# Second attention's last sums, m2, output block and first filters put in other places of a C2f-attention kernel

## The chip, the cores and the metric

The kernel runs on one NeuronCore of a Trainium2 chip. The core has five engines with queues of their own: TensorE (PE, matrix products into PSUM), VectorE (DVE) and ScalarE (ACT) for elementwise work, GpSimd (POOL), and SyncE (SP), which here only issues DMA transfers. The engines meet through semaphores. Each runs its own instructions in the order in which the program lists them, so the place of an instruction in its engine's list matters as much as what it computes. The metric is the device time of the whole program in microseconds (us).

## The reference

The input is eight images of 512 channels by 32 x 32 pixels in float32. A group norm over 32 groups is followed by a block with two inner stages, and the block's input is added at the end:

```python
def bot_attention(x, qkv_w, rw, rh):
    b, c, h, w = x.shape
    hw = h * w
    qkv = conv2d(x, qkv_w, 0).reshape(b, 3, HEADS, HD, hw)
    q, k, v = (qkv[:, 0], qkv[:, 1], qkv[:, 2])
    r = (rw + rh).reshape(1, HEADS, HD, hw)
    logits = jnp.einsum('bhdi,bhdj->bhij', q, k + r) * HD ** (-0.5)
    a = jax.nn.softmax(logits, axis=-1)
    out = jnp.einsum('bhij,bhdj->bhdi', a, v)
    return out.reshape(b, c, h, w)
...
t = cbs(x, cv1_w, cv1_bn, 0)
ys = [t[:, :C], t[:, C:]]
for i in range(N):
    yi = ys[-1]
    z = cbs(yi, m_cv1_w[i], m_cv1_bn[i], 1)
    z = bot_attention(z, m_qkv_w[i], m_rw[i], m_rh[i])
    z = jax.nn.silu(bn_eval(conv2d(z, m_cv2_w[i], 0), m_cv2_bn[i]))
    ys.append(yi + z)
return cbs(jnp.concatenate(ys, axis=1), cv2_w, cv2_bn, 0)
...
x = x + _L0_conv_ref(_gn(x), L0_conv_cv1_w, L0_conv_cv1_bn, L0_conv_cv2_w, L0_conv_cv2_bn, L0_conv_m_cv1_w, L0_conv_m_cv1_bn, L0_conv_m_qkv_w, L0_conv_m_rw, L0_conv_m_rh, L0_conv_m_cv2_w, L0_conv_m_cv2_bn)
```

Here N = 2 stages, C = 256 channels, 4 heads of 64, and `cbs` is a convolution with batch norm and SiLU. `m_cv1_w` is a 3 x 3 convolution, all others are 1 x 1.

## The kernel before

**Pairs and stages.** Images are worked on in four pairs (p = 0 to 3); call their images a and b. A pair goes through two stages n = 0 and 1. In each, a 3 x 3 convolution (`conv3x3`, in Winograd form, both images at once) is followed, for a and then for b, by the products for q, k and v ("projection"), the attention, and `m2` (the 1 x 1 convolution behind the attention, with SiLU and the addition of the stage's input). After stage 1 the output convolution cv2 of a and of b follows as a Strassen product with blocks `a1, a1_more, a2, a3` and `b1, b1_more, b2, b3`. The attention of b is called the second attention of its stage.

**Filling PE.** The group norm and the first convolution (cv1) of the next pair are done inside the present pair: cv1 of the next pair's image a within stage 0's first attention and m2, cv1 of its image b around stage 0's second attention. cv1 is cut into pieces: `begin`, `go_on`, then `rest(0)` to `rest(3)`. In pair 0 (`direct`) it is plain, with 16 profile rows (7.0 us) for each of four output blocks; later it is a Strassen product, with `begin` of 8 rows (3.5 us), `go_on` of 16 (7.1 us), and four `rest` of 8 rows. Each fp32 product counts as two rows in the profile. In the last pair parts of cv2 (`parts_of`) stand there instead.

**Attention.** `attention_fast` runs over four groups g (a 128-channel block and a half of 512 query columns), each with four pairs of key blocks: PE makes logits (`l_ps`, L960), ACT their exponentials (`pt`, L964), DVE adds up the exponentials (`acc`, L978 and L980), PE multiplies by v (`av_ps`, L994). A group's result is evacuated by ACT and a DVE addition (`z`, L1001 and L1002). The sums over partitions (`s_ps`) go through memory in `sums` and `spread`, and DVE multiplies `z` by the reciprocals `rs` (`scale`, L1066). For the second attention of stage 0 (`at_once=True`) the last group's sums are made directly in PSUM (`last_sums`, L1028), with the reciprocal of a whole 128x512 tile on DVE (L1111).

**Hooks.** The dictionary `behind` holds work to be put behind the additions of a given place: the key (g, j) is the j-th pair of group g, an integer g its first pair, NG = 4 the end of the last group and NG + 1 the place behind the last sums. The two tuples `NORM_A` and `NORM_B` say at which of these places the next pair's group norm takes its next step; the steps are statistics of the four input blocks (DVE), their mean over groups (`gm_ps`, a small PE product, L661), the inverse deviation (`gv_ps`, `gr`, L680, then three GpSimd steps up to `shift`, L681, L737, L738), and the normalisation on ACT (`x`, L744):

```python
        NORM_A = ((0, 2), (0, 3), (1, 1), (1, 2), (1, 3), 2, (2, 1), (2, 2), (2, 3), 3)
        NORM_B = ((0, 1), (0, 2), (0, 3), (1, 1), 2, (2, 1), (2, 2), (2, 3), 3, (3, 1), (3, 2), (3, 3))
```

**Preparations in pair 0.** Filters for stage 1's convolution are turned into Winograd form by `make_u` (DVE, ACT, and stores issued on GpSimd), four blocks (oc, k) from `load_late`'s taps; `more_u` steps through them, and `u_new` are the results. The position sums rw + rh are made by `make_r` (`r_new`, L206) and stored: for n = 1 in stage 0's first attention, for n = 0 in stage 1's. Convolution inputs of image a for the next stage are made in pieces by `tiles_in`; `tiles_later(1)` and `tiles_later(2)` are such pieces (`v_new`, stored by GpSimd, L1745).

**What sets the order.** A scheduler lists the instructions of each engine in program order; `tc.issue_after(x)` puts what follows behind instruction x. PSUM has three two-bank slots with the tag "big" (for logits, norm means, sums, m2 and the convolution) and one slot for `av_ps`; an operation waits until a slot's last reader is done. In `conv3x3`, ACT copies half of each result (`c_m`, L609) and DVE adds and subtracts (`c_t`, L610 and L611, to `z`, L642). In `b3` the last call, `finish(3)`, issues the output block's ACT operations (`c_out`, L460), whose stores GpSimd issues (L1263).

Of the kernel before, what the change touches and what calls it, by code (L numbers as in the profile page):

```python
# [61 lines left out]
def kernel(  # L62
# [137 lines left out]
    def make_r(n, raw):  # L200
        if raw is not None:
            nc.gpsimd.tensor_copy(planes(rw_sb[:, n]), natural(raw))
        for c in range(NM):
            for half in range(NH):
                r = act.tile([P, ROWS, F], F32, tag="t", name="r_new", bufs=4)
                nc.gpsimd.tensor_tensor(  # L206
                    r, rw_sb[:, n, c].unsqueeze(1).to_broadcast([P, ROWS, F]),
                    rh_sb[:, n, c, ts(half, ROWS)].unsqueeze(2).to_broadcast([P, ROWS, F]), ALU.add,
                )
                nc.gpsimd.dma_start(r_dram[n][c][:, ts(half, HALF)], r.rearrange("p h w -> p (h w)"))  # L210
# [245 lines left out]
    def stages(act, small, ps_big, ps_av, n_pt):  # L456
# [8 lines left out]
        shifted = [None]  # L465
# [97 lines left out]
        def conv3x3(n, vs, u_of, z, groups=G, summed=None):  # L563
# [10 lines left out]
            for oc in range(NM):  # L574
                dst = z[:, oc].rearrange("p g x -> p (g x)").rearrange("p (t r w) -> p r t w", r=4, w=F)
                for i in range(NI):
# [32 lines left out]
                    nc.scalar.copy(m24, slots(inner_ps, 1))  # L609
# [180 lines left out]
        def project_direct(n, z, w, early=None, middle=None):  # L790
# [5 lines left out]
            def qk(c):  # L796
                for which in (1, 0):
                    o = which * C + c * P
                    ps = conv1x1(
                        lambda k: w[k][:, o : o + P], lambda k, half: z[:, k, ts(half, HALF)], NM  # L800
                    )
                    if which == 0:
                        nc.scalar.copy(q[:, c], ps.rearrange("p a b -> p (a b)"))
                    else:
                        dst = img(kr[:, c])
                        rw = rw_sb[:, n, c].unsqueeze(1).to_broadcast([P, F, F])
                        rh = rh_sb[:, n, c].unsqueeze(2).to_broadcast([P, F, F])
                        tt(dst, img(ps.rearrange("p a b -> p (a b)")), rw, ALU.add)
                        tt(dst, dst, rh, ALU.add)

            qk(0)
            if early:
                early()
# [123 lines left out]
        def attention_fast(qkv, ao, at, behind, at_once=False):  # L937
# [157 lines left out]
            if not at_once:  # L1095
                with tc.issue_after(added.ins):
                    scale(g - 1, rss.pop(g - 1))
                return SimpleNamespace(
                    added=added,
# [7 lines left out]
            with tc.issue_after(added.ins):  # L1107
                scale(g - 1, rss.pop(g - 1))
# [77 lines left out]
        def m2(n, ao, yi, dst_of):  # L1186

            pss = [ps_big.tile([P, NH, HALF], F32, tag="big", name="m2_ps") for _ in range(NM)]
            for half in range(NH):
                for oc in range(NM):  # L1190
                    for k in range(NM):
                        nc.tensor.matmul(  # L1192
                            pss[oc][:, half, :], m2_sb[:, n, k, ts(oc, P)], ao[:, k, ts(half, HALF)],
                            start=(k == 0), stop=(k == NM - 1),
                        )
            for half in range(NH):
                for oc in range(NM):
                    t = act.tile([P, HALF], F32, tag="t", name="t", bufs=4)
                    m2_silu[0] = silu(t, pss[oc][:, half, :], bn_m2[n] + oc)
# [18 lines left out]
        def strassen(b, ws, top, tags, tile_of):  # L1218
# [46 lines left out]
            def part3(bottom):  # L1265
# [29 lines left out]
                finish(3, m1)  # L1295
# [296 lines left out]

    for p in range(NP):
# [23 lines left out]
        def t_qk_p():  # L1617
            if len(pairs_of_t) == 1:
                pairs_of_t.clear()
                return held("p4")  # L1620
            return t_qk()

        def next_cv1(which, xts, y1, b):
# [11 lines left out]
            f = s.strassen_cv1(take_blocks("sw", None, which, SW_NAMES), xts, y0s, y1, t_qk_p if which else t_qk)  # L1635
# [7 lines left out]


# [3 lines left out]
        feed(units(0) + (direct_keys(0) if direct else sqs(0, 0)))  # L1648
        z = new_z()
        t = s.conv3x3(0, vs, u_of(0), z, summed=None if direct else z[:, :, 0])  # L1650
# [6 lines left out]
        if direct:  # L1657
            qkv = s.project_direct(0, z[:, :, 0], [take(key) for key in direct_keys(0)])
# [9 lines left out]

        def load_late(oc, k, area):
            nc.gpsimd.dma_start(  # L1670
                area[:, : 9 * P].rearrange("p (t o) -> p t o", o=P), m_cv1_w[1, ts(k, P), :, ts(oc, P)]
            )
            return area
# [32 lines left out]
        NORM_B = ((0, 1), (0, 2), (0, 3), (1, 1), 2, (2, 1), (2, 2), (2, 3), 3, (3, 1), (3, 2), (3, 3))  # L1706
        if p == 0:
            more_u = filters([(0, 0, load_late(0, 0, inside(Y2[0])))])
            second_taps = load_late(0, 1, inside(Y2[1]))
        behind = hooks(NORM_A, (0, 1, 4, 10, 11, 12, 13, 14)) | {NG: begin_cv1(0, Y1[0], ia + 2)}  # L1710
        if p == 0:
# [7 lines left out]
            def with_r():  # L1719
                with tc.issue_after(s.shifted[0].ins):  # L1720
                    make_r(1, raw_1)
# [51 lines left out]
        else:  # L1773
# [11 lines left out]
            if direct:  # L1785
                more_u = filters(
                    [(0, 1, second_taps)] + [(1, k, load_late(1, k, late_area(tag))) for k, tag in enumerate("qk")]
                )
                with tc.issue_after(end.scaled.ins):
                    for _ in range(16):  # L1790
                        made = step_u()
# [22 lines left out]
        tiles_later(1)  # L1814
# [9 lines left out]
        def parts_of(ocs):  # L1824
# [7 lines left out]
            NG: begin_cv1(1, Y1[1], ia + 3), NG + 1: lambda: nxt.go_on()  # L1832
        }
        if not more:
# [11 lines left out]
            behind[NG] = parts_of([0])  # L1846
            behind[NG + 1] = parts_of([1])
# [9 lines left out]
        if more:  # L1857
            for i in range(4 if direct else 3):
                nxt.rest(i)
        else:  # L1860
            parts_of([2, 3])()
# [8 lines left out]
        if more and not direct:  # L1870
            nxt.rest(3)
# [11 lines left out]
        if p == 0:  # L1883
# [5 lines left out]
            behind[2] = lambda: (make_sq(0, tiles, sums), make_r(0, None))  # L1889
# [6 lines left out]
        def middle():  # L1896
            end.spread()
            end.scale()
            s.m2(1, z[:, :, 0], Y2[0], lambda oc, half: img(y3a[half][:, oc, :]))
            if more:  # L1900
# [51 lines left out]
        a3([[side(Y2[0], half), img2(y3a[half])] for half in range(NH)])  # L1952
        bottom = [[side(Y2[1], half), img2(y3b[:, half])] for half in range(NH)]
        if more:
# [9 lines left out]
            b3(bottom)  # L1964
# [116 lines left out]
```

## Time and profile before

| what | us |
|---|---|
| three runs | 2343.49, 2348.35, 2348.51 |
| median | 2348.35 |
| the profiled execution | 2349.44, with a span of 2348.0 |
| PE busy | 2237.3 (95%) |
| DVE busy | 1748.5 (74%) |
| ACT busy | 1089.3 (46%) |
| GpSimd busy | 224.8 (10%) |

The mean granted PE clock of the profiled execution is 0.986. The costliest groups of the page are these; columns are line, engine, operation, output and inputs with their shapes and count, then busy us and mean ns of one, then the idle time of the engine just ahead of them with what ended most of it:

```profile
L964 ACT ACTIVATE pt<-l_ps 128x1024 f32<-128x1024 f32 x512 | 495.7, 1023 | 361.9 <-PE l_ps L960 326.2
L980 DVE TENSOR_TENSOR acc<-acc,pt 128x1024 f32<-128x1024 f32 x384 | 474.2, 1235 | 100.4 <-ACT pt L964 77.6
L994 PE MATMUL av_ps<-pt,vT 64*64 64x512 f32 x4096 | 494.9, 601 | 11.6 <-DVE z L1002 10.5
L960 PE MATMUL l_ps<-q,kr 64*64 64x512 f32 x4096 | 489.4, 593 | 2.8 <-ACT pt L964 2.4
L604 PE MATMUL c_ps<-v_in,u 128*64 128x128 f32 x4320 | 243.7, 275 | 12.9 <-issue 10.2
```

Attention makes up the largest share of the PE time, and in it DVE's additions take almost as long as each of the two products. Three more kinds of rows appear below. A row of the timeline has start and duration in us, engine, line, operation, output and inputs, count, and in brackets the idle time ahead with what ended it; rows of the same kind that follow each other are put together, so "x2" with 2.55 is two additions. A row of the waits has the us in total, the number of waits and the longest.

### The profile page before, as it was taken

How to read it: one execution, taken by the hardware profiler on the slowest of the kernel's cores; microseconds unless marked ns; L12 is line 12 of the kernel's file. 1: busy time of each engine (PE TensorE's matmuls, PEld its weight loads, DVE VectorE, ACT ScalarE, POOL GpSimd, SP SyncE). 2: the span in 40 equal slices, each digit the busy share in tenths (PEclk: the TensorE clock that was granted, in tenths of full speed). 3: DMA queues.
4: the chain of work that ended last, by engine and by line, in shares of the span. 5: the costliest groups of instructions: out<-in, count | busy, mean ns of one | idle time of the engine just before them, and what ended most of it. 6: DMA issues, size and time to landing. Idle time of an engine off the chain costs nothing.

```text
span 2348.0 us, 40464 instructions
## 1 busy us (share of the span) xinstructions
PE 2237.3 (95%) x16338; PEld 1089.6 (46%) x16338; DVE 1748.5 (74%) x2632; ACT 1089.3 (46%) x1334; POOL 224.8 (10%) x426
## 2 busy tenths in 40 slices
PE   7898999999999999999999999999999999999997
PEld 3553437443455443734347443564345633473443
DVE  6966979768848688886857868886793867786642
ACT  7245462545224666355423665445622354335532
POOL 4103200010120000000021000000012000000002
PEclk9899999999999999999999999999999999999998
DMA  9513715321374142512158141342126611151114
GB/s 320 204 61 131 291 51 207 131 76 51 96 217 157 60 131 91 197 50 91 55 138 270 32 157 48 132 154 73 55 72 172 217 47 50 63 192 33 55 28 132
DMA packets 127892, 281.06 MB, mean 120 GB/s; under 512 B 34096, under 2 KB 55324, under 8 KB 126672
## 3 DMA queue, kind: packets, MB, share of 16 engines
q1 hardware_dynamic: 99712, 192.25, 25.2%
q0 software_dynamic: 27984, 86.13, 12.0%
q8 instruction: 131, 2.15, 0.4%
q14 instruction: 65, 0.53, 0.1%
HBM read 210.29 MB, written 68.03 MB: 119 GB/s over the span
## 4 chain that ended last, share of the span: by engine, by line
PE 71%; DVE 17%; issue 4%; DMA 2%; ACT 2%; POOL 0%; SPq 0%; DVEq 0%; ACTq 0%; POOLq 0%
PE av_ps L994 15%; PE l_ps L960 14%; PE c L1212 8%; PE c_ps L604 7%; PE c_new L1212 6%; PE p_ps L850 5%; PE m_ps L1192 4%; PE x_ps L1312 4%; PE ps L487 3%; DVE acc L980 3%; PE pv_ps L856 2%; PE s_ps L1011 1%; PE p_ps L856 1%; DVE acc L978 1%; ACT pt L964 1%
## 5 line engine op out<-in xcount | busy, mean ns | idle before, releaser
L964 ACT ACTIVATE pt<-l_ps 128x1024 f32<-128x1024 f32 x512 | 495.7, 1023 | 361.9 <-PE l_ps L960 326.2
L980 DVE TENSOR_TENSOR acc<-acc,pt 128x1024 f32<-128x1024 f32 x384 | 474.2, 1235 | 100.4 <-ACT pt L964 77.6
L994 PE MATMUL av_ps<-pt,vT 64*64 64x512 f32 x4096 | 494.9, 601 | 11.6 <-DVE z L1002 10.5
L960 PE MATMUL l_ps<-q,kr 64*64 64x512 f32 x4096 | 489.4, 593 | 2.8 <-ACT pt L964 2.4
L994 PEld LDWEIGHTS av_ps<-pt,vT 64*64 64x64 f32 x4096 | 156.5, 134 | 289.4 <-issue 240.3
L960 PEld LDWEIGHTS l_ps<-q,kr 64*64 64x64 f32 x4096 | 159.7, 134 | 275.0 <-issue 250.4
L604 PE MATMUL c_ps<-v_in,u 128*64 128x128 f32 x4320 | 243.7, 275 | 12.9 <-issue 10.2
L604 PEld LDWEIGHTS c_ps<-v_in,u 128*64 128x64 f32 x4320 | 239.2, 138 | 21.1 <-issue 18.7
L1192 PE MATMUL m_ps<-z,m_sb 128*128 128x512 f32 x256 | 112.5, 592 | 0.0
L850 PE MATMUL p_ps<-t_z,sq 128*128 128x512 f32 x224 | 106.2, 597 | 6.0 <-DVE c_t L611 5.9
L609 ACT COPY c_m<-c_ps 128x512 f32<-128x512 f32 x48 | 28.1, 585 | 176.7 <-PE c_ps L604 99.4
L978 DVE TENSOR_TENSOR acc<-pt 128x1024 f32<-128x1024 f32 x64 | 78.9, 1232 | 29.1 <-ACT pt L964 29.1
L460 ACT ACTIVATE t<-m_ps,bh,sh 128x512 f32<-128x512 f32 x64 | 46.8, 775 | 85.6 <-PE m_ps L1192 78.0
L850 PE MATMUL p_ps<-z,sq 128*128 128x512 f32 x168 | 80.5, 602 | 5.9 <-ACT z L460 5.9
L1262 POOL DMA_DIRECT2D c_out<-in_x_dram x56 | 50.4, 986 | 307.6 <-ACT c_out L460 305.2
L1192 PEld LDWEIGHTS m_ps<-z,m_sb 128*128 128x128 f32 x256 | 48.3, 190 | 58.8 <-issue 55.0
L1066 DVE TENSOR_TENSOR z<-z,rs 128x512 f32<-128x512 f32 x64 | 43.9, 686 | 30.1 <-DMA rs<-r_dram 29.9
L522 POOL MEMSET w_rows<- 128x32 f32 x48 | 7.9, 164 | 582.6 <-PE s_ps L1011 289.3
L1002 DVE TENSOR_TENSOR z<-av_ps,z 128x512 f32<-128x512 f32 x64 | 43.9, 686 | 24.8 <-ACT z L1001 24.8
L460 ACT ACTIVATE z<-z,bh,sh 128x512 f32<-128x512 f32 x64 | 46.9, 804 | 27.5 <-DVE z L642 26.8
L460 ACT ACTIVATE c_out<-cz,bh,sh 128x512 f32<-128x512 f32 x14 | 16.7, 1292 | 91.6 <-DVE cz L1289 91.6
L850 PEld LDWEIGHTS p_ps<-t_z,sq 128*128 128x128 f32 x224 | 38.9, 190 | 38.7 <-issue 29.9
(326 smaller groups left out, 3212.5 us busy)
## 6 DMA issues: line engine op xcount, KB each, us to landing
u<-u SPq DMA_DIRECT2D x135, 512.0 KB
sq<-sq SPq DMA_DIRECT2D x42, 384.0 KB
rs<-r_dram SPq DMA_DIRECT2D x118, 128.0 KB
x<-in_x_dram SPq DMA_DIRECT2D x28, 512.0 KB
r_in<-r SPq DMA_DIRECT2D x28, 512.0 KB
y_in<-y SPq DMA_DIRECT2D x28, 512.0 KB
c_out<-in_x_dram POOLq DMA_DIRECT2D x56, 256.0 KB, 5.4
out_dram<-c_out POOLq DMA_DIRECT2D x56, 256.0 KB, 4.3
```

The costliest lines, as they stand in the source:

```text
L460: silued[0] = nc.scalar.activation(dst, src, AF.Silu, scale=sh[:, k : k + 1], bias=bh[:, k : k + 1])
L487: last_product[0] = nc.tensor.matmul(ps[:, half, :], w_of(k), rhs_of(k, half), start=(k == begin), stop=(k == end))
L604: nc.tensor.matmul(to[o], us[cp][:, k, row, c, o], rhs, start=(k == 0), stop=(k == NM - 1),)
L850: nc.tensor.matmul(ps[:, o, :], w[:, o, :], rhs, start=not onto, stop=True, skip_group_check=onto)
L960: nc.tensor.matmul(ps[kh * HD : (kh + 1) * HD, hd, :], kr[r, c, o : o + HD], q[r, c, ts(half, HALF)], start=True, stop=True,)
L964: last_exp[0] = exp = nc.scalar.activation(pt, ps, AF.Exp, scale=SCALE)
L978: return nc.vector.tensor_tensor(accs[g], pt[0], pt[1], ALU.add)
L980: ins = nc.vector.tensor_tensor(accs[g], accs[g], pt[i], ALU.add)
L994: nc.tensor.matmul(avs[g][hd * HD : (hd + 1) * HD, kh, :], vT[r, j, o : o + HD], pt[i][r, hd, :], start=(j == 0), stop=(j == NJ - 1),)
L1192: nc.tensor.matmul(pss[oc][:, half, :], m2_sb[:, n, k, ts(oc, P)], ao[:, k, ts(half, HALF)], start=(k == 0), stop=(k == NM - 1),)
L1212: nc.tensor.matmul(ps[:, o, :], w[:, k, ts(o, P)], rhs[part][:, c], start=(k == 0 and not onto), stop=(k == KB - 1), skip_group_check=onto,)
L1312: nc.tensor.matmul(ps[:, o, :], w[:, c, ts(o, P)], rhs[c], start=(c == 0 and not onto), stop=(c == 1), skip_group_check=onto,)
```

## The change

- `make_r` runs on DVE instead of GpSimd, with the copies of rw into order for n = 1 on ACT (`turn_r`); for n = 0 it moves from stage 1's first attention to a place behind m2 in the projection after it, behind the evacuation of the last group.
- Pair 0's first filter block of stage 1, (1, 0, 0), is made in the first direct projection, and its taps and the next block's are loaded ahead of stage 0's convolution. In the first attention (0, 1) is made, in the part around m2 only (1, 0) and (1, 1), in 8 steps rather than 16. `tiles_later(1)` stands behind the next to last of the kr additions there.
- `NORM_B` begins one place later; the statistics' last two blocks, mean and deviation are at (0, 2), (0, 3), (1, 2), (1, 3).
- In the second attention of stage 0 the last sums come ahead of cv1's `begin`, which moves from NG to NG + 1; m2 follows it, and then `go_on` and all four `rest`. `rest(3)` no longer stands behind stage 1's convolution, and its block of sums is held in the tiles q and k. In the last pair one part of cv2 stands ahead of m2 and three behind it.
- The last-but-one group's `scale` stands behind the last evacuation (`evicted`) instead of behind the last addition.
- `b3` returns its last `finish` as a function; the next convolution calls it behind its first `c_m` copy.
- m2's PSUM tiles are one for each half instead of one for each output block.

```diff
-    def make_r(n, raw):
-        if raw is not None:
-            nc.gpsimd.tensor_copy(planes(rw_sb[:, n]), natural(raw))
+    def make_r(n):
...
-                nc.gpsimd.tensor_tensor(
+                tt(
...
-                    nc.scalar.copy(m24, slots(inner_ps, 1))
+                    copied = nc.scalar.copy(m24, slots(inner_ps, 1))
+                    if after:
+                        with tc.issue_after(copied.ins):
+                            after()
+                        after = None
...
             if early:
-                early()
+                with tc.issue_after(k_added[-1].ins):
+                    early()
...
             if not at_once:
-                with tc.issue_after(added.ins):
+                with tc.issue_after(evicted[0].ins):
                     scale(g - 1, rss.pop(g - 1))
...
-            with tc.issue_after(added.ins):
+            with tc.issue_after(evicted[0].ins):
                 scale(g - 1, rss.pop(g - 1))
...
-            pss = [ps_big.tile([P, NH, HALF], F32, tag="big", name="m2_ps") for _ in range(NM)]
+            pss = [ps_big.tile([P, NM, HALF], F32, tag="big", name="m2_ps") for _ in range(NH)]
...
-                finish(3, m1)
+                return lambda: finish(3, m1)
...
+        if p == 0:
+            with tc.issue_after(shifted.ins):
+                first_taps, second_taps = [load_late(0, k, inside(Y2[k])) for k in range(NM)]
         z = new_z()
-        t = s.conv3x3(0, vs, u_of(0), z, summed=None if direct else z[:, :, 0])
+        t = s.conv3x3(0, vs, u_of(0), z, summed=None if direct else z[:, :, 0], after=last_out)
...
+            def early():
+                for _ in make_u(1, 0, 0, first_taps, new=u_new_early):
+                    pass
+
+            qkv = s.project_direct(0, z[:, :, 0], [take(key) for key in direct_keys(0)], early=early)
...
-        NORM_B = ((0, 1), (0, 2), (0, 3), (1, 1), 2, (2, 1), (2, 2), (2, 3), 3, (3, 1), (3, 2), (3, 3))
+        NORM_B = ((0, 2), (0, 3), (1, 2), (1, 3), 2, (2, 1), (2, 2), (2, 3), 3, (3, 1), (3, 2), (3, 3))
...
-            more_u = filters([(0, 0, load_late(0, 0, inside(Y2[0])))])
-            second_taps = load_late(0, 1, inside(Y2[1]))
+            more_u = filters([(0, 1, second_taps)])
...
-                with tc.issue_after(s.shifted[0].ins):
-                    make_r(1, raw_1)
+                turn_r(1, raw_1)
+                make_r(1)
...
-                more_u = filters(
-                    [(0, 1, second_taps)] + [(1, k, load_late(1, k, late_area(tag))) for k, tag in enumerate("qk")]
-                )
+                more_u = filters([(1, 0, load_late(1, 0, inside(Y2[1]))), (1, 1, load_late(1, 1, late_area("q")))])
                 with tc.issue_after(end.scaled.ins):
-                    for _ in range(16):
+                    for _ in range(8):
                         made = step_u()
...
-        tiles_later(1)
+        with tc.issue_after(s.k_added[-2].ins) if direct else nullcontext():
+            tiles_later(1)
...
-            NG: begin_cv1(1, Y1[1], ia + 3), NG + 1: lambda: nxt.go_on()
+            NG + 1: begin_cv1(1, Y1[1], ia + 3)
...
-            behind[NG] = parts_of([0])
-            behind[NG + 1] = parts_of([1])
+            behind[NG + 1] = parts_of([0])
...
         if more:
-            for i in range(4 if direct else 3):
+            nxt.go_on()
+            for i in range(4):
                 nxt.rest(i)
         else:
-            parts_of([2, 3])()
+            parts_of([1, 2, 3])()
...
-        if more and not direct:
-            nxt.rest(3)
...
-            behind[2] = lambda: (make_sq(0, tiles, sums), make_r(0, None))
+            behind[2] = lambda: make_sq(0, tiles, sums)
...
+            if p == 0:
+                with tc.issue_after(end.evicted.ins):
+                    make_r(0)
...
-            b3(bottom)
+            last_out = b3(bottom)
```

## The prediction

> **What bounds the kernel now.** I read the page's busy shares and chain of waits, then the table of waits of TensorE (PE), then PE's timeline over the whole span, listing each gap and what ended it. A gap is worth removing only there: PE is the bound.
>
> ```profile
> PE 2237.3 (95%) x16338; PEld 1089.6 (46%) x16338; DVE 1748.5 (74%) x2632; ACT 1089.3 (46%) x1334; POOL 224.8 (10%) x426
> ...
> PE 71%; DVE 17%; issue 4%; DMA 2%; ACT 2%; POOL 0%; SPq 0%; DVEq 0%; ACTq 0%; POOLq 0%
> ```
>
> ```profile
> PE gm_ps L661 <- DVE mv L655: 14.9, 4, 8.0
> PE av_ps L994 <- DVE z L1002: 10.5, 8, 3.5
> ...
> PE s_ps L1011 <- DVE acc L980: 9.1, 7, 2.3
> PE c_ps L604 <- ACT c_m L609: 8.6, 3, 6.7
> ...
> PE pv_ps L856 <- DVE z L1002: 3.7, 5, 1.3
> ```
>
> PE is idle for about 110 us; my list of gaps of 0.3 us and more adds up to 94.5. Rows that run slower than elsewhere add about 27, nearly all just after a gap. No matmul is added or removed, so all gain must come from these two sums. Times below are microseconds, negative is a gain.
>
> The first pair's first-image attention of conv stage 1:
>
> ```profile
> 474.67 3.21 DVE L980 TENSOR_TENSOR acc<-acc,pt 128x1024 f32<-128x1024 f32 x2
> ...
> 477.67 3.10 POOL L206 TENSOR_TENSOR r_new<-rw_sb,rh_sb 128x512 f32<-128x512 f32 x2
> ...
> 477.98 3.87 DVE L980 TENSOR_TENSOR acc<-acc,pt 128x1024 f32<-128x1024 f32 x2
> ...
> 482.00 0.64 PE L1011 MATMUL s_ps<-acc,ones 128*32 128x256 f32 x8 [2.28 <-DVE acc L980]
> ...
> 484.63 3.63 PE L994 MATMUL av_ps<-pt,vT 64*64 64x512 f32 x16 [2.00 <-DVE z L1002]
> ```
>
> Two adds take 2.55 elsewhere; here 3.21 and 3.87 beside GpSimd's adds, and PE pays 2.28 + 2.00, then 1.74 of slow clock (3.63 against 1.89).
>
> The second pair's second attention, stage 0, and its end:
>
> ```profile
> 868.75 0.23 PE L661 MATMUL gm_ps<-mv,gmat 64*64 64x4 f32 x2 [2.82 <-DVE mv L655]
> ...
> 877.81 0.11 DVE L680 TENSOR_SCALAR gr<-gv_ps 128x4 f32<-128x4 f32 x1
> 878.01 1.04 POOL L681 TENSOR_TENSOR gr<-gr,mhalf 128x4 f32<-128x4 f32 x1 [29.46 <-DVE gr L680]
> ...
> 892.24 1.94 ACT L964 ACTIVATE pt<-l_ps 128x1024 f32<-128x1024 f32 x2 [0.84 <-PE l_ps L960]
> ...
> 892.76 0.54 POOL L1745 DMA_DIRECT2D v<-v_new  x1 [1.59 <-DVE v_new L560]
> ...
> 921.13 3.35 DVE L1111 RECIPROCAL rs<-rs 128x512 f32<-128x512 f32 x1
> ...
> 924.94 0.68 DVE L1066 TENSOR_TENSOR z<-z,rs 128x512 f32<-128x512 f32 x1
> ```
>
> PE waits for the statistics, `gr` follows nine microseconds later, and the last scale ends at 925.5.
>
> **The skill.** "SBUF — State Buffer", section "Who interferes with whom": a VectorE (DVE) instruction with two SBUF inputs and a GpSimd one that reads SBUF exclude each other. The trace agrees: two adds at 196.74 took 5.08 beside `r_new`. "TensorE: Matmul & The Clock Gate", Part 1: after an idle window of some 3.4 us PE runs at half rate. The trace agrees in kind (3.69 instead of 1.90 after the gap of 3.52 at 206.12), but shows the same after gaps of 2.0 (484.63), so I charge or credit 1.2 to 1.8 for any gap of over 2. "Perfetto Trace Analysis", Tensor Engine section: queues of ScalarE (ACT), DVE and GpSimd are strict FIFO; so a waiting ACT norm holds every exp behind it. No row before shows that at this size.
>
> **The change part by part.** Order of instructions comes from both programs' static orders, durations from rows of before.
>
> *First pair's position sums on DVE.* In attention a0 four `r_new` (0.6 each, as 128x512 adds) fit DVE's idle 2.19 before 196.74, and the adds there lose their 2.5 of stretching. The gap of 3.52 at 206.12 shrinks by some 2.1 and its slow clock (1.79 + 0.99) largely goes: -4 (-5.5 to -1.5). In stage 1 the four `r_new` leave the attention for the place behind m2 in the following projection: stretching there was 0.66 + 1.32 + 0.98 = 3.0; as pair 1 has no such gaps at all, 2.28 + 2.00 + 1.74 go: -6 (-6 to -1). Four adds on DVE stand before `kr` and the logits: 2.4 at most exposed, I take +1 (0 to +2.4).
>
> *First filters a stage ahead.* One `make_u` (24 DVE operations, about 9.6; 6 ACT; 9 DMA issues of 0.54 on GpSimd) moves into the first direct projection, between the two kr halves, into DVE's idle of 139.6 to 148.7: hidden, 0.5 too long. But its first two ACT operations (0.8) stand before conv's fourth `c_m` and write into a buffer that PE reads until about 118.4; that `c_m` moves from 116.85 to about 119.4, DVE's chain behind it starts 2.6 later and has 0.70 of idle to give (before 122.72), so ACT's `z` and PE's gap before 135.05 (1.64) come +1.9 (0 to +3.6). Tap loads leave 20 to 45 us, where DMA is full, for about 50 and 66: 0 (-1 to +0.5). In the second projection, DVE has eight steps instead of sixteen, `kr` starts at about 262 instead of 274.8, and ACT, behind DVE's filters, gives its copies earlier: gaps 1.80 + 1.70 + 1.09 at 263.76, 269.18, 273.99 go: -4.6 (-4.6 to -2). `tiles_later(1)` is put behind kr's adds, so kr isn't late for it: counted in that.
>
> *Statistics later in second attention (NORM_B).* Gone: gm_ps gaps of 0.80 (pair 0), 2.82 (pair 1), 2.19 + 1.69 of slow clock (pair 2). New: `gr` stands behind the v_new operations, so relative to pair 1 at 892.4 instead of 877.8; GpSimd's three steps (1.03 + 0.99 + 1.26) stand behind the third v store, which is issued until 893.3, so `shift` is there at 896.7. ACT's two norms (1.6) now stand between exp 10 and exp 11: that exp moves from 892.24 to 898.3. Behind it wait all later exps, then PE for `av` and for PSUM slots. PE's lead absorbs some 2.2: stall 3.9, and some 1.7 of slow clock where it fell in gaps before. In that stall DVE catches up, so the gaps of 0.95 + 1.01 that follow (900.80, 902.44 and the like, with 1.7 slow clock in pairs 0 and 2) go. Nets: pair 0 +5.6 - 0.8 - 1.96 - 1.7 = about +1.2 (-4.5 to +7), pair 1 +4.8 - 2.8 - 2.0 = 0 (-4.8 to +5), pair 2 +5.7 - 3.9 - 1.96 - 1.7 = -1.8 (-7.5 to +3.9). This is the least certain wait.
>
> *Second attention's end.* Sums go first, then cv1's first product (3.5), m2 (7.0), the other products (21). Gone: conv's start stalls in pairs 1 and 2 (0.43 + 0.40 + 2.92, 1.4 slow: 5.2), pair 0 (1.64), pair 3 (1.13). New in pairs 1 and 2: from PE's last `av` at 913.0, sums 1.0, product 3.5, half of m2 3.5: PE is at 921.0. DVE: last add 913.4, six input sums 3.6, `z` evacuation and scale 1.2, two w_rows and rs 1.8, one w_d 0.6, reciprocal 3.3, w_d and scale 1.2: 925.1. So +4.1, and +1.2 of clock (0 to 6). Also, with the last product no longer behind conv, PE waits for `c_t` and `z` as pair 0 does: 1.06 + 1.18 = +2.2. Net of each: 7.5 - 5.2 = +2.3 (-3 to +4). Pair 0, with 7.1 in the first product, covers DVE's 8.1: -1.6; pair 3 -1.1.
>
> *Scale behind the evacuation.* In the second pair, second projection of stage 1:
>
> ```profile
> 1060.79 0.69 DVE L1066 TENSOR_TENSOR z<-z,rs 128x512 f32<-128x512 f32 x1 [1.81 <-DMA rs<-r_dram]
> ...
> 1062.00 0.68 DVE L1002 TENSOR_TENSOR z<-av_ps,z 128x512 f32<-128x512 f32 x1
> ...
> 1062.74 1.16 PE L856 MATMUL pv_ps<-sq,z 128*128 128x128 f32 x8 [1.27 <-DVE z L1002]
> ```
>
> The scale waited for its DMA and the evacuation, ready since 1059.63, stood behind it. After, the scale comes second: pv gaps 0.52 + 1.27 + 0.43 + 0.58 + 0.92 go: -3.7 (-3.7 to -1.5).
>
> *Last output block behind next conv's first copy.* The copy at 694.09 stood behind four `c_out` (ACT; two waited for a store to free their buffer, 22.3 over the run); two go behind it, ahead of the second copy, which PE feeds only at 695.1: gaps of 1.07 + 0.84 (pair 1), 0.41, 0.63: -2.9 (-2.9 to 0). m2's accumulators by half: 0, they only free earlier (-1 to +0.5).
>
> Sum: pair 0 -4 - 6 + 1 + 1.9 - 4.6 + 1.2 - 1.6 = -12.1; pair 1 +2.3; pair 2 +0.5; pair 3 -1.1; scale -3.7, output -2.9: **-17.0**. The profiled execution took 2349.44 (span 2348.0): 2332.4. The median is 1.1 under it: **2331**.
>
> **Rivals.** *B: the norm comes in time* (exp 11 not held, as the trace shows 7 us of slack for GpSimd today): three nets become -4.5, -4.8, -7.5, together 16 better: 2315. Against it: the static order. *C: the norm's wait isn't absorbed*, 6.1 + 1.7 each time with the later gaps kept: +7, +5, +3.9, together 16.5 worse: 2348. For it: ACT is FIFO and DVE has little slack. *D, slower: the same wait, longer.* Where GpSimd's issue of stores holds `shift` beyond 6.1 + 1.7 = 7.8 us of delay in all three places, the whole gain is gone and more; at 10 us each: 2348 + 12 = 2360. Against it: GpSimd is busy for 10% of the span. *E: pair 0 gives nothing for r and filters*, because another DVE operation is late next: 12 worse, 2343.
>
> **Numbers.** Forecast 0.55, B 0.16, E 0.09, C 0.13, D 0.07. Within 0.2% (4.7 us), about what can be told from no change, lie half of E and most of C: 0.12; slower 0.08; faster 0.80. Range 2314 to 2347: it takes in B, E and the lower half of C.
>
> **What would show it.** Right: no DVE add stretched near 196 and 478; PE gaps near 482 gone; an ACT norm with several us of idle `<-POOL shift` in the second attentions of pairs 0 to 2; m2 with about 4 us `<-DVE z` in pairs 1 and 2; no stall at their conv starts. Wrong: exp rows late by over 8 us there, or new PE gaps in the first projection.

## The result, and the profile after

The changed kernel takes 2307.1 us (2304.7 to 2308.2, four runs) against 2346.8 us of the kernel before (2343.5 to 2348.5, four runs): a ratio of 0.9831, 95% interval 0.9814 to 0.9848, or 39.7 us less. The forecast had 17 us less, in a range from 2314 to 2347. The sign was right, the size less than half.

The profiled execution of the changed kernel took 2304.68 us, with a span of 2302.9. It is the fastest of its four, and the profiled one of before (2349.44) is slower than all four of its kernel, so the two traces differ by 45.1 us of span. Everything below is counted in these two traces. The page's busy shares and its chain of waits by engine:

```profile
PE 2216.4 (96%) x16338; PEld 1081.5 (47%) x16338; DVE 1750.1 (76%) x2640; ACT 1089.1 (47%) x1336; POOL 212.3 (9%) x417
...
PE 78%; DVE 13%; ACT 4%; issue 2%; DMA 2%; POOL 1%; DVEq 0%; SPq 0%; ACTq 0%; POOLq 0%
```

PE has the same 16338 instructions and is busy 20.9 us less (2237.3 - 2216.4); it is idle 24.2 us less (110.7 to 86.5). So a good part of the gain is no wait at all: the same products ran faster. Most of that is the clock of PE. This view gives, for stretches of the kernel before, busy time and count of each engine, then the granted PE clock (as a share), DMA share and GB/s:

```profile
140.00:200.00 60.00, 57.12 (x467) 24.41 (x469) 40.33 (x54) 31.91 (x37) 10.52 (x14) 1.00 0.10 34
204.80:211.60 6.80, 5.48 (x28) 1.79 (x32) 5.77 (x9) 1.32 (x3) 0.79 (x3) 0.50 0.24 86
331.10:334.50 3.40, 3.40 (x16) 1.02 (x20) 3.40 (x4) 0.12 (x1) 0.00 (x0) 0.50 0.03 2
484.70:488.10 3.40, 3.40 (x19) 0.97 (x23) 2.84 (x3) 0.00 (x0) 0.00 (x0) 0.50 0.13 40
955.70:959.10 3.40, 3.40 (x37) 3.40 (x35) 3.40 (x8) 0.00 (x0) 0.00 (x0) 0.50 0.18 37
1430.10:1433.50 3.40, 3.40 (x24) 0.75 (x20) 2.62 (x7) 2.42 (x3) 0.00 (x0) 0.51 0.03 5
1464.30:1467.70 3.40, 3.32 (x16) 1.05 (x20) 3.40 (x5) 0.21 (x1) 0.00 (x0) 0.50 0.06 14
1518.90:1522.30 3.40, 3.40 (x36) 3.40 (x34) 3.40 (x8) 0.00 (x0) 0.00 (x0) 0.50 0.07 27
1972.90:1976.30 3.40, 3.40 (x20) 1.06 (x24) 3.19 (x3) 0.37 (x1) 0.00 (x0) 0.50 0.03 2
```

Between such windows the clock is full. Each window is 3.4 us long (the first is two of them) and costs 1.7. Behind the prologue (all that stands ahead of pair 0's first projection, at 129 us) before has 30.7 us of them, after has one. The same view of the changed kernel:

```profile
904.00:907.40 3.40, 3.40 (x5) 1.35 (x4) 2.59 (x7) 0.15 (x1) 0.22 (x2) 0.50 0.00 0
1430.00:1433.40 3.40, 3.27 (x32) 1.28 (x36) 2.55 (x3) 3.40 (x6) 0.00 (x0) 1.00 0.12 28
1458.10:1461.50 3.40, 3.40 (x8) 1.59 (x9) 3.40 (x9) 0.56 (x1) 0.23 (x2) 1.00 0.00 0
```

With the prologue (23.9 against 17.1 us at half clock), the windows cost 27.3 before and 10.2 after: 17 us of the traces' difference. The 3.4 of them that lie in the prologue buy nothing, since PE is idle 3.3 us longer there. The rest is in the main waits: PE's idle time fell by 24.2 in all.

The two traces show more of the clock than is usual. The mean granted clock of the 21 executions of the kernel before that stand beside the experiments is 0.986 to 0.990, 0.988 on average; that of the changed kernel's four is 0.991 to 0.993, 0.992 on average. From these means I estimate that the clock makes some 9 of the 39.7 us.

PE's waits in the changed kernel (total us, times, longest):

```profile
PE p_ps L853 <- ACT z L458: 8.2, 7, 1.2
PE l_ps L963 <- ACT pt L967: 7.7, 7, 1.9
...
PE m_ps L1195 <- DVE z L1069: 6.2, 3, 2.5
PE av_ps L997 <- DVE z L1005: 5.0, 8, 1.3
...
PE s_ps L1014 <- DVE acc L983: 1.0, 1, 1.0
```

Gone from the list are the waits of `pv_ps` for `z` (3.7), of the projection for `c_t` (5.9), two of three waits for `c_m`; `gm_ps` for `mv` fell from 14.9 to 9.9, of which 8.1 is the start of the program. New are `m_ps` for the scaled `z` and more `l_ps` for exp: both were foreseen, at too high a price.

The stages in the two traces, from each stage's first PE product to the next one's (us, after minus before), beside the term that the prediction put there:

| step, stage | forecast | measured |
|---|---|---|
| r on DVE: pair 0, first attention of stage 0 | -4 | -4.7 |
| r on DVE: pair 0, stage 1, first attention | -6 | -4.9 |
| its cost in the second attention there | +1 | +1.5 |
| filters: prologue, first conv and projection | +1.9 | +0.3 |
| filters: around m2 and second projection | -4.6 | -3.7 |
| statistics: second attention of pairs 0, 1, 2 | +1.2, 0, -1.8 | -1.2, -1.1, -3.6 |
| second attention's end to projection, pairs 1, 2 | +2.3, +2.3 | -0.4, -2.1 |
| second attention's end and conv, pairs 0, 3 | -1.6, -1.1 | -1.8, -1.8 |
| scale behind evacuation: five projections | -3.7 | -5.3 |
| output block: conv of pairs 1 to 3 | -2.9 | -4.3 |
| first projection behind conv, five places | 0 | -6.6 |
| second attentions without a term (four) | 0 | -3.6 |
| rest | 0 | -0.3 |
| sum | -17.0 | -43.7 |

The remaining 1.4 of the span lie behind PE's last product.

How the lines shown of before look now. Pair 0, first attention of stage 1, in the changed kernel:

```profile
462.05 2.55 DVE L983 TENSOR_TENSOR acc<-acc,pt 128x1024 f32<-128x1024 f32 x2
...
464.70 2.55 DVE L983 TENSOR_TENSOR acc<-acc,pt 128x1024 f32<-128x1024 f32 x2
...
467.40 0.64 PE L1014 MATMUL s_ps<-acc,ones 128*32 128x256 f32 x8
...
469.05 1.95 PE L997 MATMUL av_ps<-pt,vT 64*64 64x512 f32 x16 [1.01 <-DVE z L1005]
```

Additions take 2.55 again where they took 3.21 and 3.87; of 2.28 + 2.00 idle 1.01 is left, and the product behind it takes 1.95 and not 3.63. Pair 1, second attention of stage 0:

```profile
869.09 0.15 DVE L682 TENSOR_SCALAR gr<-gv_ps 128x4 f32<-128x4 f32 x1
...
869.45 0.54 POOL L1750 DMA_DIRECT2D v<-v_new  x1 [1.60 <-DVE gr L682]
870.01 1.26 POOL L683 TENSOR_TENSOR gr<-gr,mhalf 128x4 f32<-128x4 f32 x1
871.35 0.40 POOL L739 TENSOR_TENSOR shift<-gm,gr 128x4 f32<-128x4 f32 x1
871.84 0.54 POOL L740 TENSOR_SCALAR shift<-shift 128x4 f32<-128x4 f32 x1
872.42 1.52 ACT L746 ACTIVATE x<-x,shift,gr 128x512 f32<-128x512 f32 x2 [5.02 <-POOL shift L740]
873.84 1.92 ACT L967 ACTIVATE pt<-l_ps 128x1024 f32<-128x1024 f32 x2
...
874.90 1.09 PE L963 MATMUL l_ps<-q,kr 64*64 64x512 f32 x8 [1.94 <-ACT pt L967]
...
895.86 4.45 PE L1195 MATMUL m_ps<-z,m_sb 128*128 128x512 f32 x10
...
898.29 3.34 DVE L1114 RECIPROCAL rs<-rs 128x512 f32<-128x512 f32 x1
...
902.10 0.67 DVE L1069 TENSOR_TENSOR z<-z,rs 128x512 f32<-128x512 f32 x1
...
902.83 4.38 PE L1195 MATMUL m_ps<-z,m_sb 128*128 128x512 f32 x6 [2.51 <-DVE z L1069]
```

The chain is the predicted one, step for step: third store, three GpSimd steps, ACT held for 5.02, the exp behind it late, PE waiting. PE's idle time is 0.47 + 1.94 (the first for `gr`, at 869.29) instead of 3.9. And m2's second half waits 2.51 for the last scale, with 0.54 ahead of the sums, instead of 4.1. Ahead of that wait PE has done ten of m2's sixteen rows (4.45), where the prediction counted half of m2 (3.5).

### The profile page after: what moved, and what is told of

It reads as the page before. It is cut to its first block, busy times and chain, and to the rows that moved or that the text cites. A ratio compares the mean times of both kernels' runs of the same rounds, so it can differ in the third digit from the quotient of the medians.

```text
span 2302.9 us, 40466 instructions
## 1 busy us (share of the span) xinstructions
PE 2216.4 (96%) x16338; PEld 1081.5 (47%) x16338; DVE 1750.1 (76%) x2640; ACT 1089.1 (47%) x1336; POOL 212.3 (9%) x417
## 3 DMA queue, kind: packets, MB, share of 16 engines
q0 software_dynamic: 27984, 86.13, 12.4%
## 4 chain that ended last, share of the span: by engine, by line
PE 78%; DVE 13%; ACT 4%; issue 2%; DMA 2%; POOL 1%; DVEq 0%; SPq 0%; ACTq 0%; POOLq 0%
PE av_ps L997 16%; PE l_ps L963 15%; PE c L1215 8%; PE c_ps L602 8%; PE c_new L1215 6%; PE p_ps L853 6%; PE ps L485 5%; PE m_ps L1195 4%; PE x_ps L1315 4%; PE pv_ps L859 2%; DVE acc L983 2%; ACT pt L967 1%; PE s_ps L1014 1%; PE p_ps L859 1%; DVE acc L981 1%
## 5 line engine op out<-in xcount | busy, mean ns | idle before, releaser
L963 PE MATMUL l_ps<-q,kr 64*64 64x512 f32 x4096 | 488.3, 591 | 10.1 <-ACT pt L967 7.7
L997 PE MATMUL av_ps<-pt,vT 64*64 64x512 f32 x4096 | 486.4, 592 | 7.5 <-DVE z L1005 5.0
L602 PE MATMUL c_ps<-v_in,u 128*64 128x128 f32 x4320 | 237.5, 273 | 0.0
L485 PE MATMUL ps<-x,w 128*128 128x512 f32 x128 | 56.1, 594 | 0.0
L1315 PE MATMUL x_ps<-t_x,sw 128*128 128x512 f32 x128 | 55.9, 592 | 0.0
```

Of the source, the lines that this page charges most:

```text
L485: last_product[0] = nc.tensor.matmul(ps[:, half, :], w_of(k), rhs_of(k, half), start=(k == begin), stop=(k == end))
L602: nc.tensor.matmul(to[o], us[cp][:, k, row, c, o], rhs, start=(k == 0), stop=(k == NM - 1),)
L963: nc.tensor.matmul(ps[kh * HD : (kh + 1) * HD, hd, :], kr[r, c, o : o + HD], q[r, c, ts(half, HALF)], start=True, stop=True,)
L997: nc.tensor.matmul(avs[g][hd * HD : (hd + 1) * HD, kh, :], vT[r, j, o : o + HD], pt[i][r, hd, :], start=(j == 0), stop=(j == NJ - 1),)
L1315: nc.tensor.matmul(ps[:, o, :], w[:, c, ts(o, P)], rhs[c], start=(c == 0 and not onto), stop=(c == 1), skip_group_check=onto,)
```

## The experiments

All stand beside the changed kernel's 2307.1 us; "slower" and "faster" are the difference of medians. Beside them the kernel before had medians of 2345.7 to 2347.7. Undoing seven parts one at a time costs 49 us in all, more than the 39.7 of the change, as it would if parts share waits; no run undoes two of them. The four executions of one kernel lie 1.6 to 5.6 us apart, those of u7_out_first 10.4.

**Why did the projection's waits for `c_t` go?** No step had them. I had charged pairs 1 and 2 with one more each. Two theories: *lag* (DVE comes late out of the convolution because the convolution began too early for it, or its first `c_m` stood behind output work), and *slots* (m2's new PSUM tiles let the product have a slot that is free). Before, the conv's end in pair 0, stage 1:

```profile
415.23 0.68 DVE L611 TENSOR_TENSOR c_t<-c_ps,c_m 128x512 f32<-128x512 f32 x1
...
416.05 1.95 PE L850 MATMUL p_ps<-t_z,sq 128*128 128x512 f32 x4 [1.06 <-DVE c_t L611]
```

and after:

```profile
402.89 0.68 DVE L613 TENSOR_TENSOR c_t<-c_ps,c_m 128x512 f32<-128x512 f32 x1
...
403.72 1.96 PE L853 MATMUL p_ps<-t_z,sq 128*128 128x512 f32 x4
```

*u5_old_end*, the second attention's end as before, with the place of `rest(3)`'s sums and the parts of cv2 in the last pair:

```diff
...
-            NG + 1: begin_cv1(1, Y1[1], ia + 3)
+            NG: begin_cv1(1, Y1[1], ia + 3), NG + 1: lambda: nxt.go_on()
...
-            nxt.go_on()
-            for i in range(4):
+            for i in range(4 if direct else 3):
...
+        if more and not direct:
+            nxt.rest(3)
```

> Second attention's end put back as before (first product ahead of the last sums, second ahead of m2, last product behind the convolution), all else as in the changed kernel. Theory lag (the waits for c_t in the projection exist because DVE comes out of the convolution late, and it is late because the convolution's inputs were made while PE already ran it): PE waits for c_t L613 come back in pairs 0 and 3 (about 1.06 each), conv start stalls of 3.8 in pairs 1 and 2 and 1.1 in pairs 0 and 3 come back, m2's waits of 2.5 go; together 5 to 9 us slower than the changed kernel. Rival slots (those waits went because m2's PSUM tiles are cut by halves): no c_t wait comes back; 2 to 5 us slower.

Measured: 2312.3, 5.2 slower, and its waits of PE:

```profile
PE c_ps L602 <- issue: 7.1, 4, 2.9
...
PE p_ps L853 <- DVE c_t L613: 2.4, 2, 1.2
```

*u7_out_first*, the last output block ahead of the copy:

```diff
-            last_out = b3(bottom)
+            b3(bottom)()
```

> Last output block issued ahead of the next convolution again, all else as in the changed kernel. Theory lag: c_m waits of 3.2 in all in pairs 1 to 3 come back, and with them c_t waits of about 1.1 in the three projections behind: 7 to 10 us slower than the changed kernel. Rival slots: c_m waits alone, 3 to 5 us slower.

Measured: 2315.2 (2309.3 to 2319.7), 8.1 slower:

```profile
PE c_ps L602 <- ACT c_m L607: 10.4, 3, 7.3
...
PE p_ps L853 <- DVE c_t L613: 2.7, 3, 1.2
```

*u8_m2_by_block*, m2's tiles by output block:

```diff
-            pss = [ps_big.tile([P, NM, HALF], F32, tag="big", name="m2_ps") for _ in range(NH)]
+            pss = [ps_big.tile([P, NH, HALF], F32, tag="big", name="m2_ps") for _ in range(NM)]
...
```

> m2's PSUM tiles one for each output block again, all else as in the changed kernel. Theory lag: within 1 us of the changed kernel, no c_t wait. Rival slots: c_t waits in five projections come back, 5 to 7 us slower.

Measured: 2315.8, 8.7 slower, and no wait of `p_ps` for `c_t`. So lag owns the `c_t` waits: two return in pairs 0 and 3 with the old end, three in pairs 1 to 3 with the old output place, none with m2's old tiles. But both theories missed u8's time. Its trace shows what the halves do. m2 in pair 0, stage 1, of u8:

```profile
494.96 7.03 PE L1195 MATMUL m_ps<-z,m_sb 128*128 128x512 f32 x16
...
500.31 0.78 ACT L458 ACTIVATE t<-m_ps,bh,sh 128x512 f32<-128x512 f32 x1 [7.09 <-PE m_ps L1195]
...
511.39 1.09 PE L963 MATMUL l_ps<-q,kr 64*64 64x512 f32 x8 [0.69 <-DVE q L923]
```

and of the changed kernel:

```profile
493.43 7.03 PE L1195 MATMUL m_ps<-z,m_sb 128*128 128x512 f32 x16
...
497.06 1.45 ACT L458 ACTIVATE t<-m_ps,bh,sh 128x512 f32<-128x512 f32 x2 [5.38 <-PE m_ps L1195]
```

The first SiLU comes 3.6 us after m2's start instead of 5.4: a tile of one half is complete after four of m2's eight products (3.5 us), one of an output block after six (5.3 us). DVE ends m2's additions 9.2 us after m2's start instead of 10.4, ahead of the next attention's `kr` and `q`. In u8 PE's products behind m2 also stand in another order, so no run tells how much the SiLU does alone. In u8's trace idle time comes back in the attentions behind m2 (0.4 to 1.0 us in five stages), with two more clock windows there, and a third in a stage whose idle time was no longer than before. Of the 8.7 the trace shows 7.9 up to PE's last product. The table's lines without a term are in good part this: in u8 the four second attentions without a term are 0.63, 0.63, 0.35 and 0.19 longer (the other 1.7 there is before's window at 1972.87), and each of the five projections of the scale 0.24, without idle time.

**Is the scale's place worth 3.7?** *u6_scale_first*:

```diff
-            with tc.issue_after(evicted[0].ins):
+            with tc.issue_after(added.ins):
                 scale(g - 1, rss.pop(g - 1))
```

(in both places where it stands.)

> Last-but-one scale behind the last addition again (ahead of the evacuation), all else as in the changed kernel. Theory: pv_ps waits for z come back in the five projections of stage 1 and pair 3, some 3.7 us, with small gaps after them: 3 to 7 us slower than the changed kernel. Rival (the evacuation was late for another reason, and the order is nothing): within 1.5 us.

Measured: 2317.2, 10.1 slower, over the range. The waits of `pv_ps` for `z` are back as expected:

```profile
PE m_ps L1195 <- DVE z L1069: 8.8, 3, 3.9
...
PE pv_ps L859 <- DVE z L1005: 5.2, 5, 1.4
```

The rest is in the first line: with the new end of the second attention, m2 stands close behind the sums, and a scale that waits for its DMA ahead of the evacuation makes m2 late (2.0 us in pair 1, 2.9 in pair 2 with its clock window). Another window, in pair 2's second attention, costs 1.4. With the new end the scale's place is worth more than its own 3.7; what it is worth with the old end, no run shows.

**Position sums, filters, statistics.** *u1_r_on_gpsimd*:

```diff
...
-                tt(
+                nc.gpsimd.tensor_tensor(
...
-            behind[2] = lambda: make_sq(0, tiles, sums)
+            behind[2] = lambda: (make_sq(0, tiles, sums), make_r(0, None))
...
```

> Position sums made by GpSimd in their old places again, all else as in the changed kernel. Theory contention (GpSimd's additions stretch DVE's, and DVE's lateness is PE's gap): additions of 2.5 take 3 to 5 again beside r_new, PE gaps of 2 to 3.5 return in the first pair's two first attentions, the first pair's stage 1 second attention gets 1.5 shorter; 5 to 10 us slower than the changed kernel. Rival (DVE has room there now, since the filters have gone elsewhere): under 3 us.

Measured: 2311.8, 4.7 slower, a little under the range; the stages are as expected (+3.7 and +6.2 in the two first attentions, -2.1 in the second of stage 1, -1.7 around m2). The stretched additions of its trace, beside GpSimd's rows:

```profile
467.21 3.10 POOL L206 TENSOR_TENSOR r_new<-rw_sb,rh_sb 128x512 f32<-128x512 f32 x2
...
467.53 3.87 DVE L985 TENSOR_TENSOR acc<-acc,pt 128x1024 f32<-128x1024 f32 x2
```

*u2_filters_late*:

```diff
...
-            qkv = s.project_direct(0, z[:, :, 0], [take(key) for key in direct_keys(0)], early=early)
+            qkv = s.project_direct(0, z[:, :, 0], [take(key) for key in direct_keys(0)])
...
-            more_u = filters([(0, 1, second_taps)])
+            more_u = filters([(0, 0, load_late(0, 0, inside(Y2[0])))])
+            second_taps = load_late(0, 1, inside(Y2[1]))
...
-                    for _ in range(8):
+                    for _ in range(16):
```

> First filter block made in the first attention again, the others behind it as before, all else as in the changed kernel. Theory: PE gaps of 1.8, 1.7 and 1.1 return in the first pair's second projection, and DVE's lateness in the first attention; 3 to 7 us slower than the changed kernel. Rival (ACT and DVE had room, the gaps came from the order of kr alone, which is kept): under 1.5 us.

Measured: 2315.2, 8.1 slower, a little over the range: the stage around m2 is 9.8 longer, with a wait of 3.9 for ACT's `ypad` and 6.8 us at half clock; the convolution ahead is 1.0 shorter.

*u4_norm_early*, the old tuple of `NORM_B`:

> Second attention's statistics in their old places, all else as in the changed kernel. Theory gain (the new wait of ACT for shift costs less than the waits it replaced): gm_ps waits of 0.8, 2.8 and 2.2 and the pairs of 1.0 behind them return in pairs 0 to 2, the l_ps waits of 0.5 + 1.9 go: 3 to 9 us slower than the changed kernel. Rival, the prediction's own step (the new wait costs about as much as it saves): within 2.5 us.

Measured: 2311.5, 4.4 slower. In the stages: +1.1, +1.3, +2.5 in the three attentions, of which the idle time is -0.2, +1.6 and +1.1, and a clock window stands in the first and the third. So in idle time the new order is cheaper by only 2.5 in all, where the prediction's sum has nothing (three times 3.9, less 2.8, 4.8 and 4.2); these two windows make 3.4 more.

**Do the new waits cost because an engine is full, or by its order?** *v12_norm_sums_later*:

```diff
-                    calls[key] = [step_norm] if key in norms else []
+                    calls[key] = [step_norm] * norms.count(key)
...
-        NORM_B = ((0, 2), (0, 3), (1, 2), (1, 3), 2, (2, 1), (2, 2), (2, 3), 3, (3, 1), (3, 2), (3, 3))
+        NORM_B = ((0, 2), (0, 3), (1, 2), (1, 3), (2, 2), (2, 3), 3, 3, (3, 1), (3, 1), (3, 2), (3, 3))
...
-            nxt.sums()
+            with tc.issue_after(end.scaled.ins):
+                nxt.sums()
```

> The changed kernel with two more shifts: in the second attention each normalisation step from (2, 2) on (two of them doubled) instead of from 2 on, and cv1's six input sums on DVE behind the last scale. Theory (both new waits are DVE's and GpSimd's order, not their load): l_ps waits of 1.9 on ACT go in pairs 0 to 2, m2's waits of 2.5 go in pairs 1 and 2, 7 to 13 us faster than the changed kernel. Rival (ACT or DVE is full there and the wait comes back at the next product): within 3 us of the changed kernel.

Measured: 2294.75 (2293.95 to 2296.4), 12.4 faster, and 0.9782 of the kernel before (0.976 to 0.9804), whose interval doesn't reach that of the changed kernel. Its waits:

```profile
PE l_ps L963 <- ACT pt L967: 1.8, 4, 1.1
...
PE m_ps L1195 <- DVE z L1069: 1.5, 3, 0.5
```

`l_ps` for exp fell from 7.7 to 1.8, m2's wait from 6.2 to 1.5, and behind the prologue no clock window is left. In its trace the three second attentions are 1.0, 1.7 and 1.7 shorter and their ends in pairs 1 and 2 3.8 (with the window) and 2.1. It was order. This is the best version found.

Three tries on top of it. *v3_last_pair_tiles*:

```diff
...
+            behind[0, 2] = lambda: tiles_later(1)
...
```

(in the last pair, in place of the call ahead of the attention.)

> v12_norm_sums_later with the last pair's first piece of the next convolution's input made behind the additions of (0, 2) of the second attention instead of ahead of it. Theory (in the last pair DVE makes these inputs ahead of the first additions, so exp's buffers come free late): the gaps of 1.5, 0.7 and 1.3 there go, 2.5 to 4.5 us faster than v12_norm_sums_later. Rival (DVE's backlog only moves to the end of group 1): within 1 us.

Measured: 2296.1. Its stage is 2.6 shorter in the trace, as the theory has it, but the runs (2292.6 to 2296.6) don't tell it from v12_norm_sums_later. *v4_norm_a_later*, with `NORM_A` in pair 0 as ((0, 2), (0, 3), (1, 1), (1, 2), 2, (2, 1), (2, 2), (2, 3), 3, (3, 1)):

> v3_last_pair_tiles with the first pair's first attention taking mean and deviation one place later. Theory: gm_ps's wait of 1.8 at 186 us goes, 1.5 to 3.5 us faster than v3_last_pair_tiles. Rival (shift comes later, and the norms on ACT hold an exp back): 1 us faster to 2 us slower.

Measured: 2297.3 (2295.3 to 2298.6), 1.2 slower than v3_last_pair_tiles, which the runs don't tell apart; in the trace the first attention is 1.9 longer. The wait of 1.8 at 186 us is gone, but the norms hold ACT for 3.6 and a wait of 2.4 for `z` comes at 206. The rival holds: later is no rule. *v5_last_product_behind*, with `for i in range(4 if direct else 3)`, `nxt.rest(3)` behind the convolution and its sums where they were before:

> v3_last_pair_tiles with cv1's last product behind stage 1's convolution again in pairs 1 and 2. Theory (the lag that needed all products ahead of the convolution is some 4 us, and 17.5 of filler are enough): p_ps's waits for z of 1.2 go in pairs 1 and 2, no conv start stall, about 2.3 us faster than v3_last_pair_tiles. Rival: the convolution's start waits for its inputs again, 1 to 6 us slower.

Measured: 2301.6, 5.5 slower than v3_last_pair_tiles. The convolution waits 1.8 at its start in pairs 1 and 2 and the projection 0.9 more: 17.5 us of products ahead of it aren't enough there, 21 are.

**What does a wait cost in clock?** *dw_scale_delayed*:

```diff
+            idle = act.tile([P, HALF], F32, tag="rs", name="idle", bufs=4)
+            for _ in range(4):
+                extra = tt(idle, rs, rs, ALU.add)
+            with tc.issue_after(extra.ins):
+                scaled = scale(g, rs)
...
```

> The changed kernel with four additions of 0.6 into an unused tile ahead of the last scale of each attention that ends with last sums (five of them); with what the scheduler puts between them the last scale comes 2.4 to 3.9 us later. m2's waits become 3.6 in pair 0's first attention and 5 to 6.4 in pairs 1 and 2, 0 to 3 in the other two: 10 to 14 us of idle PE time. Theory clock by chance (a stall of 2 us starts a window of half clock now and then, one of 5 us always): one window of 3.4 us, 1.7 us lost, in each of four places, 15 to 22 us slower than the changed kernel. Rival (a window needs more than that): 10 to 14 us slower, no window more.

Measured: 2312.8, only 5.7 slower. In pairs 1 and 2 the last scale does end later, 15.2 us after the start of the last sums instead of 11.5, but the scheduler put eight rows of cv1 (3.7 us) between m2's halves on PE, and the wait is 2.67 instead of 2.51. So it made only one of the waits that it was meant to make: pair 0's first grew from 1.19 to 3.86, no other by more than 1.0. Its waits:

```profile
PE m_ps L1200 <- DVE z L1069: 11.0, 5, 3.9
```

Behind the 3.86 there is a window of half clock that the changed kernel doesn't have, behind one 2.67 there is one and behind the other none, and one of three stalls of 1.95 has one. The count over all 14 traces of this study, behind the prologue (a window that begins within a few us of the stall's end): all 6 stalls of over 3 us have one, 17 of 29 of 2 to 3 us, 6 of 49 of 1.5 to 2 us. Two stalls close together count twice in this, so it is rough.

The traces allow a sharper count. Within one execution all windows lie on one grid of 3.413 us (last section). Cut each of the 14 traces at its own grid, from 130 us to PE's last product, and add up PE's idle time in each cut at full clock: of the 36 cuts with 1.86 us of idle time or more, 35 are followed by half clock; of the 8788 with less, one is (1.79). The 1.86 is read off these same traces, and no run was made to try it. Two gaps in one cut add up: 0.95 + 1.01 ahead of before's window at 331.05. So it is not the length of one stall but the idle time that falls between two points of the grid, and where a stall of 2 to 3 us falls differs from execution to execution.

## Why the prediction was wrong

**What failed is the price of the clock and of the new waits.** The working says "so I charge or credit 1.2 to 1.8 for any gap of over 2", and then charged the stalls of 1.9 to 4 that it added as surely as it credited those that it removed: three second attentions stand in its sum at 5.6, 4.8 and 5.7, of which 3.9 each is idle time and 4.4 in all clock, and two m2 waits have 1.2 of clock each. Measured: in these five places the changed kernel has one window (u1 and u2, with the same five stalls to 0.01 us, also one; u7 and dw_scale_delayed, with much the same, two). So the change gained all that before lost behind the prologue (15.4) and paid 1.7. In the sum the clock's credits were 1.9 + 1.7 + 1.7 + 1.7 + 1.7 + 2.8 = 11.5 and its charges 6.8, about 5 net against 13.7 measured: 9 of the missing 27. Part of this is luck of the two profiled executions, by the mean clocks above. The idle time of the five new waits was over-priced as well: 19.9 was booked (three times 3.9, twice 4.1), and 13.3 came (three times 2.41, twice 3.05): 6.6 more.

**The stall for the norm** was priced at "3.9, and some 1.7 of slow clock"; it was 2.4 and none. The chain was right, and the third store stood where the prediction had it, 0.36 behind `gr`. But GpSimd's three steps took 1.26, 0.40 and 0.54, for which the prediction took 1.03, 0.99 and 1.26: 1.1 less. The exp was about 5 late instead of 6.1. m2's wait, "+4.1, and +1.2 of clock", was 2.5 + 0.5, with a window in one of two.

**The wait for `c_t`** is the step whose mechanism was wrong. "With the last product no longer behind conv, PE waits for `c_t` and `z` as pair 0 does: 1.06 + 1.18" took pair 0's wait as a property of the place. It was the end of a lag that the same change removes, by making the convolution's inputs ahead of it (u5) and its first copy ahead of the output block (u7). So it didn't come in pairs 1 and 2, and went in five other places: 6.6 us that no term had. Undoing the two parts brings 5.8 of it back (2.6 in u5's trace, 3.2 in u7's). Only the wait for `z` (1.17) came.

**m2's halves** "0, they only free earlier (-1 to +0.5)": undoing them costs 8.7 in the runs. They do more than free a buffer earlier: a tile that is complete earlier moved the SiLU, and with it DVE and the next attention.

**The first `c_m`.** "+1.9 (0 to +3.6)" took PE's end with the buffer as 118.4; ACT's operation ran at 116.22 and the `c_m` moved from 116.85 to 117.14, by no more than PE's own rows there. The gap of 1.64 stayed at 1.63.

What held: r on DVE, within 1.1 us in each stage; the filters (-3.7 for -4.6); the old stall at the convolution's start; `pv_ps` (3.7 of idle time gone; of the 1.6 more in these five projections, 1.2 belong to m2's halves by u8); that the waits that take the place of others are for exp behind `shift` and for m2. Of the rivals, C, D and E fell: of all added costs only r's additions in stage 1 were dearer than booked, by 0.5. B's sign was right, but not its reason: the norm did not come in time.

## What to carry to other kernels

A wait at the end of a stage may be a lag that began at the stage's start: before it is booked as lasting, follow the late engine back to where it fell behind. Where a bound engine also changes its clock, price a wait by the idle time that can gather within one window (3.4 us here): removing long waits, or two that stand close together, gives back more than their idle time, and short new ones that stand apart cost little more than theirs. After such a change list the new waits and shift what stands ahead of them on their engine: two moves in the order gave another 12 us here.

## What was not expected of the hardware

Half clock comes in windows of 3.413 us, or whole multiples, on a fixed grid within one execution: the starts of before's 13 windows, taken by that length (3.4133), agree within 0.02 us, and the grid's position differs from execution to execution. The Trainium skill's "TensorE: Matmul & The Clock Gate", Part 1, has such a window of activity and asks for an idle one. Here no whole window had to be idle: behind 35 of 36 windows with 1.86 us of idle time or more half clock followed, behind one of 8788 with less. A stall of 2 to 3 us brought it in about half of the cases because the grid cuts some of them in two: the changed kernel's 2.51 at 902.83 lies with 2.25 in one window and was followed by half clock, its 2.51 at 1458.06 is cut into 1.40 + 1.11 and was not. Why it takes just this much the runs don't show.
